# Values through two queues, short chunks on ScalarE, a reordered pool: one core's layernorm, attention and low-rank layer

## The chip, the cores and the metric

The kernel runs on one core of a Trainium2 chip. The metric is the time of one execution on the device in microseconds (us); lower is better. "The profile" is one execution recorded by the hardware profiler: a page of summaries, and a trace that can be asked about single engines, lines and stretches. Engines are called PE (TensorE, the matrix engine; PEld its weight loads), DVE (VectorE), ACT (ScalarE), POOL (GpSimd) and SP (SyncE, which here does nothing but issue transfers, called DMAs). A "q" behind the name (ACTq, SPq) marks what an engine's sequencer does itself, such as issuing a DMA.

## The reference

```
x  = hidden_states                      # 4 sequences, 512 tokens, 1024 wide, float32
xn = layernorm(x)
out = x + attention(xn) + lora(xn)

attention: qkv = xn @ w_qkv             # 32 query heads, 8 key/value heads, 128 wide
           scores = q.k * scale - slope[head] * sqrt(distance), causal
           out = softmax(scores) @ v, then @ w_o
lora:      xn @ W.T + b + (one of four nested ranks, chosen for each token
           by a gate's softmax) xn @ A[:r].T @ B[:, :r].T
```

All is computed in float32.

## The kernel before

The kernel has three stages. `project` (to about 1146 us) normalises the tokens, projects them to queries, keys and values, and in its gaps prepares sums of the output weights. `attend` (about 1146 us to 1765 us with the passage that follows it) computes the attention. `finish` multiplies attention's output and the normalised tokens by their weights and adds everything up. The large products of the first and the last stage follow a scheme of seven products in place of eight, on two levels (the functions named `inner`, `outer`, `Inner`, `Outer`); it is paid for with sums and differences of quarters of the operands, on DVE and POOL, and with scratch tensors in device memory (`s_d`, `t_d`, `m_d`, `c_d`).

**Order.** In `project` (after its start) PE, SP, DVE and POOL, and in `attend` all five engines, execute their instructions exactly in the order in which the program writes them. An instruction that waits therefore holds up everything behind it on its engine, and that goes for DMAs too: a DMA is an instruction of the engine that issues it, and it waits there.

**The weights' sums in `project`.** `weights_put_by` is a generator, three of which run by turns in slots of the projection (a slot is one call of `beside`, about one group of four products). It loads a piece through ACT's queue (`load`, L788, its DMAs at L794, L801 and L804), waits 8 slots (L822), issues four differences on POOL or DVE as slots are free (`busy`, L810), waits 4 slots (L829), issues the store on SP (L836) and waits 6 slots. The tiles are called `wr`. POOL also makes the sums of weights that PE is about to use (`ti_q`, `ti_kv`), in the same queue.

**Attention.** There are 32 units (2 pairs of sequences, 8 key/value heads, 2 sequences of a pair). A unit holds the 4 query heads of its group and takes 4 steps; the loop in L1217 runs T over 128 steps and some more. With n and q the unit and the quarter of step T, the steps do, in this order:

- `load` (q = 0, SP): keys and queries of unit n+1.
- `values` (q = 2, L1030): the values of unit n, four DMAs of 256 KB that put the same data on four groups of 32 partitions, all on SP (L1035). The tiles `vx` and `vy` alternate between units, so unit n's values take the place of unit n-2's.
- `distances` (q = 2, when a new head begins at unit n+1, which is at odd n): the bias, one activation on ACT (L1027).
- `settle` (q = 2, L1120): four copies on ACT (L1127) take unit n-2's products out of four PSUM banks into `o`. The same four banks hold the next unit's.
- `scores` (L1047): four products of queries and keys on PE (L1053, `psc`), for each DVE's bias and minimum (L1058) and ACT's exp with its sum (L1061). A step has two rows of queries, and each is cut in a long and a short chunk; `rows` (L1039) yields them as k = 0 to 3, the odd ones short (32 to 256 columns), the even ones long (512 to 288).
- `scaled` (L1071), for the step before: POOL multiplies the four chunks by the inverse sums.
- `turn` (L1077), for two steps before: DVE transposes the probabilities into `ptx` or `pty`.
- `weigh` (L1113), for six steps before: PE multiplies them with the values (L1100, `po`).
- `aside` (L1191): pieces of the sums over a finished pair's outputs. `outer_sums` makes `os` from `o`; `middle_sums` makes further sums in `ot1`, `ot5` or `ot7` and stores all to `s_d` by SP (L1172 to L1186). The sums named (1, 2), (5, 6, 3) and (7, 4) are for different products of the last stage.

At T = 112 (L1226) the first operands of the last stage are loaded by SP, and from T = 128 PE begins its first products.

**The passage.** The last pair (`last`) is summed by DVE and POOL after the loop (L1262 to L1272); its sums take the buffers `ot5` and `ot7` again, which must first have been stored for the pair before. Its (5, 6, 3) and (7, 4) sums are stored through POOL's queue (L1168).

**Buffers.** A pool lays its tiles out in the order in which they are first asked for (L1215 for attention's; its `p`, `vx` and `ptx` lie in a pool of their own). When attention's pool is closed, the last stage's pool `c2` (L1437 to L1445) takes the same memory, and a tile there must wait for the last user of the bytes below it. Counted in KB from the start of the pool, attention's order gives `o` 0 to 24, `ot7` to 30, `ot5` to 39, `os` (two) to 63, `ot1` to 71, `vy` to 79, `pty` to 97. The last stage's gives `x` 0 to 16, `btb`, `um` and `lw` to 30, `r4` (eight) to 62, `t4` (two) to 67, `u` (two) to 75, `m1`, `m5` and `m6` (two each) to 81, `wz` to 91. `u` holds the copies of the first four products (L1394), to which the next ones are added; `t4` is the fourth sum of weights (L1343).

Of the kernel before, what the change touches and what calls it, by code (L numbers as in the profile page):

```python
# [12 lines left out]
F32 = mybir.dt.float32  # L13
AF = mybir.ActivationFunctionType
ALU = mybir.AluOpType
# [7 lines left out]
P = 128  # L23
# [43 lines left out]
def kernel(  # L67
# [13 lines left out]
    nc = tc.nc  # L81
    B, S, H = x.shape
    DOUT = wt.shape[1]
# [3 lines left out]
    NP = B // 2  # L87
    HS = S // 2
    SCALE = D ** -0.5
    KB = 5  # L90
    C = P // G
# [273 lines left out]
    def project(attention):  # L365
# [5 lines left out]
        with pool("a") as sb, tc.tile_pool(name="stats", bufs=2, reuse_waits="tile") as stats:  # L371
# [20 lines left out]
            def buf(tag, name):  # L392
                where = ar if tag in ("w0", "x11", "xi1", "x12", "xi2") else sb
                return where.tile([P, *sizes[tag]], F32, tag=tag, name=name, bufs=counts.get(tag, 1))
# [110 lines left out]
            V, GP = nc.vector, nc.gpsimd  # L505
# [131 lines left out]
            def own_sums():  # L637
                return pace[2] - pace[5] in OWN
# [145 lines left out]
            def weights_put_by(turn):  # L784

                def load(key):  # L788
                    w = buf(f"wr{turn}", "wr_" + "_".join(str(k) for k in key))
                    if len(key) == 3:  # L790
                        kp, e, j = key
                        v = w.rearrange("p (k c) n -> p k c n", k=2)
                        for c in range(2):
                            pin(nc.scalar.dma_start(  # L794
                                out=v[:, :, c], in_=rows_of(kp, ds(c * S + j * HS, HS))[:, :, e]
                            ))
                    else:
                        kp, i = key
                        if i in SUMMED:
                            src = t_d[:, SUMMED[i], :, :, kp].rearrange("p e j n -> p (e j) n")  # L800
                            pin(nc.scalar.dma_start(out=w, in_=src))  # L801
                        else:
                            k, c = {1: (0, 0), 2: (1, 0), 3: (1, 1)}[i]
                            pin(nc.scalar.dma_start(  # L804
                                out=w.rearrange("p (e j) n -> p e (j n)", e=2),
                                in_=rows_of(kp, ts(c, S))[:, k],
                            ))
                    return w

                def busy(eng):  # L810

                    held = pace[2] > pace[4] if eng is GP else own_sums()
                    return held or taken.get(eng, -9) > pace[2] - 2

                yield from pause(9 * turn)
                for n in range(turn, len(pieces), 3):
                    key, eng = pieces[n], (GP, V)[n % 2]
                    if len(key) == 2 and key[1] in SUMMED:
                        while not put_by >= {(key[0], e, j) for e in range(2) for j in range(2)}:
                            yield  # L820
                    w = load(key)
                    yield from pause(8)  # L822
                    for k, u, v in ((0, 1, 0), (1, 3, 1), (3, 3, 0), (2, 2, 3)):
                        while busy(eng):
                            yield
                        taken[eng] = pace[2]
                        pin(sub(eng, w[:, k], w[:, u], w[:, v]))
                        yield
                    yield from pause(4)  # L829
                    if len(key) == 3:  # L830
                        kp, e, j = key
                        dst = t_d[:, :, e, j, kp]
                    else:
                        kp, i = key
                        dst = m_d[i][:, :, kp]
                    pin(nc.sync.dma_start(out=dst, in_=w))  # L836
                    put_by.add(key)
                    yield from pause(6)
# [5 lines left out]
            def pause(n):  # L844
                for _ in range(n):
                    yield
# [124 lines left out]
    def attend(front, begin):  # L971
# [3 lines left out]
        with ExitStack() as stack:  # L975
            sb, sp, sq = None, None, early.__enter__()
# [14 lines left out]
            def buf(tag, name):  # L991
                where = sq if tag in queries else sp if tag in passing else sb
                return where.tile([P, *sizes[tag]], F32, tag=tag, name=name, bufs=counts.get(tag, 1))

            Q, K, V, O, bias = {}, {}, {}, {}, {}
# [22 lines left out]
            for g in range(G):  # L1018
                nc.gpsimd.affine_select(
                    out=dist[ts(g, C)], in_=dist[ts(g, C)], compare_op=ALU.is_ge, fill=FAR,  # L1020
# [9 lines left out]
            def values(u):  # L1030
                p, h, bi = u
                V[u] = buf("v" + "xy"[bi], f"v_{label(u)}")
                src = v_d[2 * p + bi, h - h % 2][h % 2].rearrange("k g c d -> k (g c) d")
                for g in range(G):
                    nc.sync.dma_start(out=V[u][ts(g, C)], in_=src)  # L1035

            PR, TOT, PT, PO, OS = {}, {}, {}, {}, {}

# [31 lines left out]

            def scaled(T):  # L1071
                for k, row, n in rows(T):
                    nc.gpsimd.tensor_scalar(  # L1073
                        row, row, TOT[T][:, k : k + 1], 1.0, ALU.mult, ALU.mult
                    )

            def turn(T):  # L1077

# [53 lines left out]
            last = (NP - 1, NKV - 1)  # L1132
# [20 lines left out]
            def middle_sums(p, h, which, of, t, kept):  # L1153


                g = len(which)
                a = t.rearrange("p (g e) (r k) -> p g e r k", g=g, r=2) if of == "o" else t.rearrange(
                    "p g e (r k) -> p g e r k", r=2
                )
                a11, a12, a21, a22 = [a[:, :, e, r] for r in range(2) for e in range(2)]  # L1160
                n = f"{p}_{h}_{which[0]}"
                m = buf(f"ot{which[0]}", f"ot_{n}").rearrange("p (s g) k -> p s g k", g=g)
                s1, s2, s4 = [m[:, k] for k in range(3)]
                s3 = m[:, 3] if kept else a21
                eng = nc.gpsimd if of == "o" and not kept else nc.vector
                kb, kp = divmod(h + 2, KB)

                queue = nc.gpsimd if (p, h) == last and not kept else nc.sync  # L1168
                d = [s_d[i][:, :, p, kb, kp] for i in which]
                if kept:  # L1170
                    for k in range(g):
                        nc.sync.dma_start(out=d[k][:, 0:4:2], in_=a[:, k, :, 0])  # L1172
                        nc.sync.dma_start(out=d[k][:, 3], in_=a[:, k, 1, 1])
                add(eng, s1, a21, a22)
                yield
                sub(eng, s2, s1, a11)
                yield
                sub(eng, s4, a12, s2)
                yield
                sub(eng, s3, a11, a21)  # L1180
                for k in range(g):
                    if kept:
                        nc.sync.dma_start(out=d[k][:, 1], in_=s3[:, k])
                    else:
                        queue.dma_start(out=d[k][:, :4], in_=a[:, k].rearrange("p e r k -> p (e r) k"))
                    queue.dma_start(out=d[k][:, 4:], in_=m[:, :3, k])  # L1186
                yield

            beside, below = deque(), deque()

            def aside(steps, times):  # L1191
                while steps and times:
# [15 lines left out]
            sb = stack.enter_context(pool("b"))  # L1208
# [3 lines left out]
            ordered.__enter__()  # L1212
            strict[0] = True

            for tag in "o ot7 ot5 os ot1 p vx vy ptx pty".split():  # L1215
                buf(tag, f"lay_{tag}")
            for T in range(STEPS + 6):  # L1217
                n, q = divmod(T, NQ)
# [9 lines left out]
                if part == 0 and done >= 0:  # L1228
                    u = p, h, bi = units[done]
# [29 lines left out]
            settle(units[-1], slice(0, 1))  # L1259
            aside(below, 99)  # L1260
            p, h = last
            cuts = [(ALL, slice(HS, S)), (ALL, slice(0, HS))]  # L1262
            sums = outer_sums(p, h, nc.vector, cuts)
            for k in range(8):
# [11 lines left out]
    def rows_of(kp, col):  # L1276

        return wt_v[:, kp, :, :, col] if kp < 2 else wo_v[:, kp - 2, :, :, col]
# [7 lines left out]
    def pin(instruction):  # L1286
        return instruction if strict[0] else tc.keep_in_program_order(instruction)
# [132 lines left out]
    def finish(sb, homes, ops, begun):  # L1420
# [14 lines left out]


        for tags, shape, n in (  # L1437
            ("x", [NP, 2, HS], 4), ("btb", [DOUT], 1), ("um", [NP, S], 1), ("lw", [12, P], 1),
            ("r4", [2, NP, HS], 8), ("t4", [KB, P], 2), ("u", [2, NP, HS], 2),
            ("m1 m5 m6", [HS], 2), ("wz", [2 * KB, HS], 1), ("sa10z sa11z", [KB, HS], 1),  # L1440
            ("s2 s4", [KB, HS], 2), ("t3", [KB, P], 2),
        ):
            for tag in tags.split():
                rank = tag in ("btb", "um", "lw")
                sb.tile([RMAX + 1 if rank else P, *shape], F32, tag=tag, name=f"lay_{tag}", bufs=n)  # L1445
# [346 lines left out]
```

## Time and profile before

| | us |
|---|---|
| median of 3 runs | 2530.39 |
| lowest and highest | 2528.26, 2533.35 |
| the profiled execution, its own time | 2529.27 |
| its span, first to last instruction | 2527.5 |

| engine | busy us | share of the span | instructions |
|---|---|---|---|
| PE | 2450.1 | 97% | 16096 |
| DVE | 1802.9 | 71% | 3586 |
| ACT | 516.0 | 20% | 1558 |
| POOL | 1929.3 | 76% | 2078 |

The page has the span in 40 slices of 63 us each; a digit is the busy share of a slice in tenths, 9 meaning 90% or more. A row of an engine's order of time gives the start in us, the length in us, the engine, the line of the kernel, the operation, what it writes and reads, how many of one kind were merged, and in square brackets the idle time before it with what ended that. The mean clock that PE was granted is 0.991 of full speed in this execution; there are stretches with 0.50.

### The profile page before, as it was taken

The numbers are of one execution on the slowest core, as the hardware profiler recorded it, in microseconds if no ns is written. First come the engines' busy times: TensorE is split into PE (matmuls) and PEld (weight loads), VectorE is DVE, ScalarE is ACT, GpSimd is POOL, SyncE is SP. The second block draws the span as 40 slices with busy tenths as digits, with TensorE's granted clock in tenths as the row PEclk, the third lists the DMA queues.
The fourth block names the chain that finished last, engine by engine and source line by source line (L and its number), as shares of the span: only waits on it lengthen the run. The fifth ranks groups of instructions, "written<-read, shape, count | busy, mean of one in ns | idle before, by whom it ended". The sixth has DMA issues, their size and how long they took to land.

```text
span 2527.5 us, 44178 instructions
## 1 busy us (share of the span) xinstructions
PE 2450.1 (97%) x16096; PEld 2082.3 (82%) x16096; DVE 1802.9 (71%) x3586; ACT 516.0 (20%) x1558; POOL 1929.3 (76%) x2078
## 2 busy tenths in 40 slices
PE   7999999999999999999999999997999999999999
PEld 6878888888888888887777777775888888888887
DVE  7776677778666676757899998975765666656574
ACT  3111111110000000116666666641000000000000
POOL 4578787887688898875999999975775667747583
PEclk9999999999999999999999999998999999999999
DMA  4389998878977777746899999999887877879884
GB/s 146 109 246 318 281 323 253 271 220 245 323 226 241 217 243 223 247 136 183 248 319 326 319 331 320 321 304 356 317 317 268 327 288 289 307 267 329 312 325 149
DMA packets 513834, 681.90 MB, mean 270 GB/s; under 512 B 155817, under 2 KB 424489, under 8 KB 499410
## 3 DMA queue, kind: packets, MB, share of 16 engines
q1 hardware_dynamic: 441554, 591.64, 71.5%
q10 hardware_dynamic: 70752, 82.85, 9.9%
q0 software_dynamic: 1312, 4.59, 0.5%
q8 instruction: 128, 2.10, 0.3%
q14 instruction: 88, 0.72, 0.1%
HBM read 417.89 MB, written 261.10 MB: 269 GB/s over the span
## 4 chain that ended last, share of the span: by engine, by line
PE 67%; DMA 3%; POOL 2%; DVE 1%; SPq 1%; issue 1%; ACT 0%; ACTq 0%; DVEq 0%; POOLq 0%
PE pc L1371 16%; PE po L1100 11%; PE psc L1053 10%; PE pd L1371 8%; PE pc_q L569 7%; PE pa L1371 4%; PE pd_q L569 3%; PE pc_kv L569 3%; PE pa_q L569 2%; PE pd_kv L569 2%; DMA sa<-s 1%; PE pa_kv L569 1%; POOL t L140 1%; POOL ti_q L140 1%; PE pc L1635 1%
## 5 line engine op out<-in xcount | busy, mean ns | idle before, releaser
L1100 PE MATMUL po<-pt,v 32*128 32x256 f32 (+7 forms) x6144 | 300.1, 334 | 5.1 <-DMA v<-v 4.4
L1061 ACT ACTIVATE p<-p,low 128x512 f32<-128x512 f32 (+15 forms) x512 | 261.4, 517 | 203.7 <-DVE low L1058 195.7
L1100 PEld LDWEIGHTS po<-pt,v 32*128 32x128 f32 x6144 | 266.1, 186 | 36.3 <-issue 23.7
L1073 POOL TENSOR_SCALAR p<-p,tot 128x512 f32<-128x512 f32 (+15 forms) x512 | 264.3, 534 | 41.3 <-DVE tot L1069 40.8
L1053 PE MATMUL psc<-k,q 128*128 128x512 f32 (+15 forms) x1024 | 279.4, 417 | 3.0 <-DVE low L1058 2.5
L140 POOL TENSOR_TENSOR t<-w 128x640 f32<-128x640 f32 x95 | 187.9, 1978 | 120.9 <-DMA w<-m 54.6
L1058 DVE CUSTOM_DVE_ANT_0 p<-psc,bias 128x512 f32<-128x512 f32 (+15 forms) x512 | 205.6, 435 | 69.5 <-PE psc L1053 66.1
L1053 PEld LDWEIGHTS psc<-k,q 128*128 128x128 f32 x1024 | 171.5, 191 | 96.6 <-issue 55.8
L140 POOL TENSOR_TENSOR t<-w,t 128x640 f32<-128x640 f32 x95 | 194.8, 2051 | 33.9 <-PE pc L1371 30.2
L140 POOL TENSOR_TENSOR wr<-wr 128x256 f32<-128x256 f32 x220 | 174.6, 795 | 47.2 <-DMA wr<-in_w_o_dram 21.6
L569 PE MATMUL pc_q<-xi,ti_q 128*128 128x256 f32 x640 | 167.6, 385 | 3.0 <-DVE q L137 2.7
L1084 DVE STREAM_TRANSPOSE pt<-p 128x1088 f32<-128x1088 f32 x128 | 167.0, 1305 | 1.7 <-POOL p L1073 1.7
L140 POOL TENSOR_TENSOR ti_q<-w_q 128x256 f32<-128x256 f32 x128 | 105.3, 822 | 67.7 <-PE pc_q L569 37.4
L140 DVE TENSOR_TENSOR wr<-wr 128x256 f32<-128x256 f32 x220 | 139.5, 634 | 14.0 <-DMA wr<-in_wt_dram 9.1
L569 PEld LDWEIGHTS pc_q<-xi,ti_q 128*128 128x128 f32 x640 | 121.4, 192 | 24.3 <-issue 4.9
L569 PE MATMUL pd_q<-xi,ti_q 128*128 128x256 f32 x448 | 117.6, 386 | 14.6 <-POOL ti_q L140 14.6
L179 ACT COPY m<-pc 128x256 f32<-128x256 f32 x30 | 11.2, 372 | 564.1 <-PE pc L1371 545.1
L1371 PE MATMUL pc<-s,t 128*128 128x256 f32 x480 | 113.3, 384 | 10.5 <-DVE m L137 10.5
L140 POOL TENSOR_TENSOR ti_q<-to_q 128x256 f32<-128x256 f32 x96 | 76.8, 800 | 47.5 <-PE pc_q L569 45.0
L1371 PE MATMUL pc<-sa,w 128*128 128x256 f32 x480 | 112.1, 381 | 0.1
L1371 PEld LDWEIGHTS pc<-s,t 128*128 128x128 f32 x480 | 92.4, 193 | 23.6 <-issue 10.9
L1371 PE MATMUL pd<-s,t 128*128 128x256 f32 x480 | 111.5, 379 | 0.0
(344 smaller groups left out, 5731.1 us busy)
## 6 DMA issues: line engine op xcount, KB each, us to landing
sa<-s SPq DMA_DIRECT2D x98, 640.0 KB, 7.9
s<-ot SPq DMA_DIRECT2D x107, 384.0 KB, 6.1
m<-wr SPq DMA_DIRECT2D x70, 512.0 KB, 4.1
w<-m SPq DMA_DIRECT2D x28, 1280.0 KB, 8.1
w_q<-in_w_qkv_dram SPq DMA_DIRECT2D x16, 2048.0 KB, 11.3
q<-q SPq DMA_DIRECT2D x32, 1024.0 KB, 5.7
v<-v SPq DMA_DIRECT2D x128, 256.0 KB, 5.9
s<-os SPq DMA_DIRECT2D x45, 512.0 KB, 6.1
```

Of the source, the lines that this page charges most:

```text
L140: return eng.tensor_tensor(dst, u, v, ALU.subtract)
L179: nc.scalar.copy(dst, alike(src, dst))
L569: nc.tensor.matmul(dst, ops_w[m][:, c, :], XI[i][m][:, c, :], start=start and c == 0, stop=c == 1, skip_group_check=True,)
L1053: nc.tensor.matmul(sc[:, :n], Q[u][:, n // C - 1].rearrange("p g k -> p (g k)"), K[u][:, :n], start=True, stop=True,)
L1058: nc.vector.tensor_tensor_reduce(row, sc[:, :n], bias[p, h][:, S - n :], -SCALE, BIG, ALU.add, ALU.min, low)
L1061: nc.scalar.activation(row, row, AF.Exp, bias=low, scale=-1.0, accum_out=TOT[T][:, k : k + 1])
L1073: nc.gpsimd.tensor_scalar(row, row, TOT[T][:, k : k + 1], 1.0, ALU.mult, ALU.mult)
L1084: nc.vector.transpose(dst, PR.pop(T).rearrange("p s (t k) -> p s t k", k=C))
L1100: nc.tensor.matmul(PO[u, g][:, to : to + n * C].rearrange("p (n k) -> p n k", k=C), V[u][ts(g, C), b % G * NT + b // G], x[:, :, :C], star ...
L1371: nc.tensor.matmul(bk, w[:, k], x[:, k], start=start and k == 0, stop=stop and k == KB - 1, skip_group_check=True,)
L1635: nc.tensor.matmul(bk, low["w"][:, c, d], low["u"][:, p, ts(r, HS)], start=start, stop=False, skip_group_check=True,)
```

## The change

Six places change.

1. The pauses of `weights_put_by`: 10 slots instead of 8 between load and first difference, 2 instead of 4 between the last difference and the store.
2. `values`: the DMAs for g = 1 and g = 3 go out on ACT's queue, those for g = 0 and g = 2 stay on SP's.
3. `scaled`: the short chunks (odd k) are multiplied by ACT (an activation with a scale per partition), the long ones by POOL as before.
4. `middle_sums` of the last pair: for (5, 6, 3) and (7, 4) the sums lie in a tile called `spare`, which takes the place of `pty` after its last use, in place of `ot5` and `ot7`. Their stores go through ACT's queue for (7, 4) and SP's for (5, 6, 3), instead of POOL's.
5. Attention's pool is laid out in another order. By the sizes in the code this gives `o` 0 to 24, `os` to 48, `pty` to 66 (of which `spare` takes 15 KB, to 63), `vy` to 74, `ot7` to 80, `ot5` to 89, `ot1` to 97.
6. `btb` grows by 1 KB, which moves everything behind it in `c2` by as much: `r4` is 31 to 63, `t4` to 68, `u` to 76, `m1` to 78, `m5` to 80, `m6` to 82, `wz` to 92.

```diff
@@ weights_put_by
-                    yield from pause(8)
+                    yield from pause(10)
                     for k, u, v in ((0, 1, 0), (1, 3, 1), (3, 3, 0), (2, 2, 3)):
...
-                    yield from pause(4)
+                    yield from pause(2)
@@ values
                 for g in range(G):
-                    nc.sync.dma_start(out=V[u][ts(g, C)], in_=src)
+                    (nc.sync, nc.scalar)[g % 2].dma_start(out=V[u][ts(g, C)], in_=src)
@@ scaled
                 for k, row, n in rows(T):
-                    nc.gpsimd.tensor_scalar(
-                        row, row, TOT[T][:, k : k + 1], 1.0, ALU.mult, ALU.mult
-                    )
+                    by = TOT[T][:, k : k + 1]
+                    if k % 2:
+                        nc.scalar.activation(row, row, AF.Identity, scale=by)
+                    else:
+                        nc.gpsimd.tensor_scalar(row, row, by, 1.0, ALU.mult, ALU.mult)
@@ middle_sums
-                m = buf(f"ot{which[0]}", f"ot_{n}").rearrange("p (s g) k -> p s g k", g=g)
+                m = spare.pop(which[0]) if (p, h) == last and which[0] in spare else buf(
+                    f"ot{which[0]}", f"ot_{n}"
+                )
+                m = m.rearrange("p (s g) k -> p s g k", g=g)
...
-                queue = nc.gpsimd if (p, h) == last and not kept else nc.sync
+                queue = nc.scalar if (p, h) == last and not kept and of == "o" else nc.sync
@@ attend
-            beside, below = deque(), deque()
+            beside, below, spare = deque(), deque(), {}
...
-            for tag in "o ot7 ot5 os ot1 p vx vy ptx pty".split():
+            for tag in "o os pty vy ot7 ot5 ot1 p vx ptx".split():
                 buf(tag, f"lay_{tag}")
...
             aside(below, 99)
             p, h = last
+            rest = sb.tile([P, 15, HS], F32, tag="pty", name="spare")
+            spare.update({5: rest[:, :9], 7: rest[:, 9:]})
@@ finish
-            ("x", [NP, 2, HS], 4), ("btb", [DOUT], 1), ("um", [NP, S], 1), ("lw", [12, P], 1),
+            ("x", [NP, 2, HS], 4), ("btb", [DOUT + HS], 1), ("um", [NP, S], 1), ("lw", [12, P], 1),
```

## The prediction

> **What bounds the kernel now.** I read the slices first, then the stages, then the engines' order of time at the two places that decide. The page:
>
> ```profile
> PE   7999999999999999999999999997999999999999
> ACT  3111111110000000116666666641000000000000
> POOL 4578787887688898875999999975775667747583
> DMA  4389998878977777746899999999887877879884
> ```
>
> TensorE (PE) is full but for slice 28. The stages, in which the columns after the window are its length, PE, weight loads, VectorE, ScalarE, GpSimd, clock, DMA share, GB/s:
>
> ```profile
> 1206.00:1640.00 434.00, 434.00 (x5601) 338.40 (x5600) 392.45 (x1099) 268.47 (x912) 429.77 (x551) 1.00 1.00 312
> 1640.00:1765.00 125.00, 102.54 (x1043) 82.52 (x1041) 79.55 (x158) 36.35 (x119) 81.86 (x92) 0.90 1.00 328
> ```
>
> Steady attention (the first row) is bound by PE, with no idle time. GpSimd is as full by chance: no PE wait names it there. The second row, the end of attention and the passage to the last stage, holds 22 us of idle PE. So anything that holds PE back in the first row adds to the span one for one, and only the second row, and some gaps of the projection (60 to 1146 us, PE 1056.48 of 1086), can give time back.
>
> Where PE is next to waiting is seen at the settling (L1127), four copies of a unit's products out of PSUM. ScalarE, then PE:
>
> ```profile
> 1451.69 0.39 ACT L1061 ACTIVATE p<-p,low 128x128 f32<-128x128 f32 x1
> ...
> 1452.76 2.05 ACT L1127 COPY o<-po 128x512 f32<-128x512 f32 x4 [0.60 <-PE po L1100]
> 1454.67 0.65 ACT L1061 ACTIVATE p<-p,low 128x384 f32<-128x384 f32 x1
> ```
> ```profile
> 1450.35 2.40 PE L1100 MATMUL po<-pt,v 32*128 32x256 f32 x48
> 1452.68 2.10 PE L1053 MATMUL psc<-k,q 128*128 128x384 f32 x8
> 1454.71 2.46 PE L1100 MATMUL po<-pt,v 32*128 32x256 f32 x48
> ```
>
> PE ends a unit's weighted values at 1452.68; the copies run to 1454.81; PE wants the same four banks for the next unit at 1454.71, the fourth in its fourth product. The slack is nothing: what delays the copies delays PE.
>
> **The change, part by part.**
>
> *Values by turns.* Two of each unit's four loads (L1035) go from SyncE's queue to ScalarE's. values(units[n]) stands at the head of step 4n+2, before distances() and settle(), and ScalarE runs its instructions in that order. The new loads must wait until PE has read the old values (of unit n-2), which is the very end of po that the settling waits for. Behind them stand the bias (L1027, when n is odd), the four copies, the exps; behind the copies stands PE. The trace shows no such load on ScalarE; the nearest row is a pair of its weight loads:
>
> ```profile
> 519.85 0.92 ACTq L794 DMA_DIRECT2D wr<-in_w_o_dram  x2
> ```
>
> I take 0.90 us a pair. Below, SyncE's shortest is 0.302 each (0.68 with the gaps); above, SyncE's in the backlog of attention is 3.50 for four, 1.8 a pair. I stay near the first: ScalarE's queue is empty in attention. A cost of nothing is only possible if the pair goes out before PE is done; that is rival A. Where n is odd, the bias, today hidden behind PE's last products, comes after the pair too:
>
> ```profile
> 1643.03 0.71 ACT L1027 ACTIVATE bias<-dist,slope 128x512 f32<-128x512 f32 x1
> 1643.76 2.05 ACT L1127 COPY o<-po 128x512 f32<-128x512 f32 x4
> ```
>
> It takes 0.71, less the 0.09 by which neighbours overlap (the exp of 0.39 is followed after 0.30), less 0.04 that shows already (these copies begin 0.13 after PE's end at 1643.63, the others 0.09): it adds 0.58. Units 2 to 31 are concerned: 16 without a bias at 0.90 are 14.4; 14 with one (odd n, 3 to 29) at 1.48 are 20.7. **+35 us** (bounds: 30x0.68+14x0.58 = 29; 30x1.8+14x0.58 = 62). Each gap stays below 1.5, and such gaps didn't bring the half clock: after 1.49 us idle at 570.99 four products still took 1.03.
>
> *Short chunks on ScalarE.* Eight activations a unit, 32 to 256 columns. I price them by the exps of those sizes (306 ns to 495, mean 0.41): 3.2 us of a unit's 17.4, in which ScalarE works 10.8 now. They stand behind the exps of the next step; in the step before a settling they have 32 and 64 columns, some 0.45 us with overlap, and the exps end 0.5 us before PE (1452.17, 1452.68): nothing. VectorE's transpose, which reads them, comes a step later. GpSimd loses rows of 290 to 693 ns (32 to 256 columns; 114 us in all), which nobody waited for in the steady part: nothing. If this cover fails, each 0.1 us at a settling is 3 us.
>
> *The stall at step 118.* PE waited for values once, behind the first loads for the last stage and six stores on SyncE:
>
> ```profile
> 1643.63 2.10 PE L1053 MATMUL psc<-k,q 128*128 128x384 f32 x8
> 1650.18 6.91 PE L1100 MATMUL po<-pt,v 32*128 32x256 f32 x48 [4.44 <-DMA v<-v]
> 1657.02 3.90 PE L1053 MATMUL psc<-k,q 128*128 128x320 f32 x8
> ```
>
> It costs 4.44 idle, then 4.5 and 1.8 us at half the clock (granted 0.50 from 1652 to 1660): 10.7. After: SyncE issues two loads, not four (2.87 us become 1.4), and PE comes 0.9 later, so some 2.1 us of idle are left, with perhaps half of the slow clock's 6. **-6** (bounds 0 and -10.7).
>
> A rule speaks here. The Trainium skill, "TensorE: Matmul & The Clock Gate", section "Why this matters for your kernels", allows no idle gap over about 3 us; by it the shrunken gap would keep the full clock, and the sum would be 3 us lower. Another speaks against the move: "DMA: Bandwidth & Descriptors", section "Issuing engines are not separate DMA queues", says that a second issuing engine saves issue time alone, not transfer time. By it the values still land behind the same bytes (DMA share 1.00 here), the stall stays, and the sum is 6 higher. I go between, since the trace shows both queues long (issues of 2 to 5 us) and engines full.
>
> *Last pair's sums in the probabilities' buffer, pool reordered.* The passage now:
>
> ```profile
> 1745.78 4.20 PE L1371 MATMUL pc<-s,t 128*128 128x256 f32 x10 [10.51 <-DVE m L137]
> ...
> 1760.67 4.63 PE L1371 MATMUL pc<-sa10y,t 128*128 128x256 f32 x10 [6.38 <-DVE m L137]
> 1765.41 2.94 PE L1371 MATMUL pc<-sa,w 128*128 128x256 f32 x10
> ```
>
> The first wait is for u (L1394), held to 1744.80 by the store of ot1, whose place it takes. After, u lies on the values (free at 1721), but ScalarE first issues the (7,4) stores, which wait for GpSimd's four ot7 sums (1730 to 1736, then four issues, 1738), and m1 lies on ot7, whose last store lands at about 1740 (GpSimd waits for it at 1740.01 today): PE goes on at 1740.5, 5 earlier. The second wait is t4 on os (VectorE's product waits until 1759.45); t4 now lies on the probabilities and is free: gone. What is late next is the following product's load (sa, issued 1744.66, landed 1765.4, by the chain of waits). Before it 4.5 MB of stores and 3.2 MB of loads must pass either way. They now start without a hole (310 GB/s in 1735 to 1750, against 407 after 1750: some 4 us), but the 2.7 MB of (5,6,3) stand ahead of the loads on SyncE's queue, and PE would idle there some 10 us and start at half clock. **-4** (bounds -12: all but the time of the bytes; +5: the queue order loses more than the hole gives).
>
> *Pauses 8/4 to 10/2* (L822, L829). Each weight sum is issued two slots (two groups of four products, 2x0.86 us) later after its load, the store at the same slot. The waits that it bears on are GpSimd's 21.6 us for wr (once 12.5, which idled PE 7.67 us at 691 and halved the clock for 10.2) and VectorE's 4.54 at 129 (PE 3.23). Cut by 1.7 each, with the second's slow clock spared: 5. SyncE, which waits 138.5 us for GpSimd in these stores, waits longer, and its later loads with it. **-4** (bounds -18: both events gone; +8: one new stall like that at 691).
>
> The sum: 35 - 6 - 4 - 4 = +21 on the profiled execution's 2529.27: **2550 us**. That execution lies 1.1 below the median of the runs (2530.39), so I leave the number there.
>
> **Rivals.**
>
> A, *the settling isn't held* (faster): the pair of loads leaves ScalarE before PE's end, and only the gains are left: 2529.3 - 14 = 2515. It decides if the loads' wait is met, or their issue done, before 1452.7 in the row above. For it: ScalarE has 0.5 us free there. Against it: the loads wait for the same products as the copies, and SyncE is seen waiting for PE at L1035 15 times, 30.4 us.
>
> B, *issues slow as SyncE's in the backlog*: +62 in place of 35 and the same gains, 2529.3 + 62 - 14 = 2577; with short chunks late at a settling, more. For it: DMA share 1.00, and ScalarE's single issues reach 1.18 us at L794. Against it: their median is 0.46.
>
> C, *the added time is given back*: a slower PE lets the stores drain, so that the passage's idle and half clock (some 25 us) go with the stall's 10.7: 35 - 36 = -1, 2529 us. For it: DMA share 1.00 up to 1765. Against it: the passage is a chain of sums, stores and loads that starts when attention ends.
>
> **Chances.** The forecast 0.61 (its own range 2533 to 2570), A 0.16, B 0.12, C 0.11. A run can tell about 0.2% (5 us) from no change. Faster: A and a third of C, 0.20. Within: most of C and the forecast's lower edge, 0.09. Slower: the rest, 0.71. The range leaves out A's lower part (0.1) and B's upper (0.08): 2516 to 2580.
>
> **What would show it.** Right: PE waiting for ScalarE's o (L1127) at L1100, some 0.9 and 1.5 us by turns, 30 times; two issues of L1035 on ScalarE just ahead of each settling; a unit every 18.5 us instead of 17.4; fewer than 4 us idle for values at step 118; no wait of ScalarE for the store of ot at L1394. Wrong: units still 17.4 us apart (A); issues of over 1 us on ScalarE (B); PE nearly without idle time between 1650 and the last stage (C). A new wait of PE for GpSimd's ti in the projection would make the pauses' term wrong.

## The result, and the profile after

The changed kernel takes 2670.57 us in the median of 4 runs (2665.72 to 2674.51), the kernel before 2529.94 beside it: a ratio of 1.0553, 95% interval 1.0533 to 1.0574. It is slower by 5.5%, some 140 us. I had said 2550, and 2580 at most. The profiled execution of the changed kernel is the one of 2665.72 us, with a span of 2664.0. Below, line numbers are those of the kernel shown in each case; the changed kernel's are up to 7 higher than before's (the weighing is L1102 there, the settling L1129).

The slices of the page, after:

```profile
PE   7999999999999999999898989888699999999999
ACT  3111111101000101176565656552000000000000
POOL 4687887877788888745565656555466567755593
PEclk9999999999999999999898989899799999999999
DMA  4389998879878777466878787887988878878884
```

PE is no longer full in most of slices 20 to 29. In slices 20 to 26 POOL has fallen from 9 to 5 or 6, and the granted clock changes between 8 and 9. The stages (columns as in the prediction), steady attention and then its end with the passage:

```profile
1200.00:1640.00 440.00, 394.31 (x4428) 309.30 (x4424) 316.66 (x868) 262.52 (x882) 256.72 (x277) 0.90 0.77 246
1730.00:1905.00 175.00, 132.06 (x1334) 107.18 (x1333) 105.30 (x218) 59.58 (x198) 84.79 (x77) 0.86 0.84 277
```

In the first row PE, which had no idle time before, is idle for 46 of 440 us, its mean clock is 0.90, and it has done a fifth fewer products in the same time (10.1 per us against 12.9). The transfers are less busy, not more: 0.77 of the engines' time against 1.00. So nothing is short of bandwidth; something holds PE. By stage, from the starts and ends of PE's products in the two traces:

| stretch | before, us | after, us | difference |
|---|---|---|---|
| up to the first `psc` of attention | 1140.8 | 1133.2 | -7.6 |
| attention, first `psc` to last `po` | 580.7 | 716.0 | +135.3 |
| last `po` to PE's last product | 801.5 | 810.4 | +8.9 |

Nearly all of it lies in attention. The waits of PE and of ACT (what waited, for what: us in all, times, longest):

```profile
PE po L1102 <- ACT o L1129: 70.8, 17, 6.4
PE pc L1378 <- DMA sa<-s: 15.1, 1, 15.1
```
```profile
ACT bias L1027 <- DMA s<-ot: 71.2, 13, 6.1
```

The first is the wait for the settling that I expected, but at 4 to 6 us a time and not at 0.9 and 1.5. The last names what ACT waited for ahead of it: a *store* of sums, which neither the bias nor the settling reads. Two units in ACT's order of time, an even one and the odd one behind it:

```profile
1428.27 0.78 ACTq L1035 DMA_DIRECT2D v<-v  x2
1429.15 2.06 ACT L1129 COPY o<-po 128x512 f32<-128x512 f32 x4 [1.13 <-PE psc L1053]
1446.61 5.22 ACTq L1035 DMA_DIRECT2D v<-v  x2
1451.88 0.72 ACT L1027 ACTIVATE bias<-dist,slope 128x512 f32<-128x512 f32 x1 [5.51 <-DMA s<-ot]
1452.51 2.03 ACT L1129 COPY o<-po 128x512 f32<-128x512 f32 x4
```

In the even unit the two loads take 0.78, a little less than the 0.90 that I had priced. In the odd unit they take 5.22, and the bias and the copies stand behind them. PE beside it:

```profile
1430.09 3.47 PE L1102 MATMUL po<-pt,v 32*128 32x256 f32 x48
...
1446.40 2.10 PE L1053 MATMUL psc<-k,q 128*128 128x384 f32 x8
1453.13 5.39 PE L1102 MATMUL po<-pt,v 32*128 32x256 f32 x48 [4.62 <-ACT o L1129]
```

After the even settling the weighing takes 3.47 in place of 2.46: 1.0 later. After the odd one PE is idle for 4.62, and then the same 48 products take 5.39, of which 1453 to 1456.9 at half the clock (granted 0.50). What the second load waited for is told by the chain of what ended last, and by SP's order of time:

```profile
1445.99 1.18 DVE ot L140
1447.17 0.02 issue
1447.18 0.32 SPq L1188
1447.50 0.04 issue
1447.55 3.96 DMA s<-ot
1451.50 0.02 issue
1451.52 0.31 ACTq L1035
```

DVE ends the last of the (1, 2) sums, SP stores them, and when the store has landed (1451.50) ACT's second load goes out (1451.52). The trace's semaphore events show why. Every DMA of SP and ACT raises, when it lands, one of eight semaphores (counters that an engine can wait for), which in these kernels are given out in turn over both queues; and an issue first waits until the DMA before it on the same semaphore has landed. The store issued at 1447.55 raises number 100. ACT's second load also raises number 100, and waits for it. The two have nothing to do with each other; they are eight transfers apart in the order in which the numbers are given out. That order is not the text's: `values` writes its four loads one behind the other, but ACT's two have numbers 116 and 100 here, with two of SP's stores (117 and 118) between them. In the last 14 of the 16 odd units it is this store (L1191) that the second load follows, and in each of the 14 the load goes out 0.02 us after the store has landed.

**Theory 1**, then: a load moved to ACT's queue brings along a wait for an older transfer of SP's, through the shared semaphore; in odd units that transfer is a store just issued; ACT's order puts the settling behind it; and a gap of 4 us makes PE run at half clock after it. Rivals: **2**, the pool's new order (`vy` beside other tiles) makes the wait; **3**, the short chunks make ACT late; **4**, two issues on ACT, or the traffic of two queues, cost this by themselves.

### The profile page after: what moved, and what is told of

Read it like the earlier page. It is cut to its first block, busy times and chain, and to the rows that moved or that the text cites. A ratio compares the mean times of both kernels' runs of the same rounds, so it can differ in the third digit from the quotient of the medians.

```text
span 2664.0 us, 44380 instructions
## 1 busy us (share of the span) xinstructions
PE 2516.1 (94%) x16096; PEld 2137.2 (80%) x16096; DVE 1807.2 (68%) x3586; ACT 595.7 (22%) x1814; POOL 1795.6 (67%) x1812
## 4 chain that ended last, share of the span: by engine, by line
PE 65%; DMA 5%; DVE 3%; SPq 2%; POOL 1%; issue 1%; ACT 1%; ACTq 0%; POOLq 0%; DVEq 0%
PE pc L1378 15%; PE po L1102 11%; PE psc L1053 8%; PE pd L1378 7%; PE pc_q L569 7%; PE pa L1378 4%; PE pd_q L569 3%; PE pc_kv L569 3%; DMA s<-ot 2%; PE pa_q L569 2%; PE pd_kv L569 2%; DVE pt L1086 1%; PE pa_kv L569 1%; DVE p L1058 1%; DMA sa<-s 1%
## 5 line engine op out<-in xcount | busy, mean ns | idle before, releaser
L1102 PE MATMUL po<-pt,v 32*128 32x256 f32 (+7 forms) x6144 | 357.6, 357 | 70.9 <-ACT o L1129 70.8
L1102 PEld LDWEIGHTS po<-pt,v 32*128 32x128 f32 x6144 | 316.3, 200 | 111.8 <-ACT o L1129 82.2
L1077 POOL TENSOR_SCALAR p<-p,tot 128x512 f32<-128x512 f32 (+7 forms) x256 | 150.7, 602 | 237.9 <-DVE tot L1069 225.2
L1053 PE MATMUL psc<-k,q 128*128 128x512 f32 (+15 forms) x1024 | 290.2, 429 | 3.0 <-DVE low L1058 2.5
L1053 PEld LDWEIGHTS psc<-k,q 128*128 128x128 f32 x1024 | 177.9, 197 | 99.8 <-issue 60.3
L1378 PEld LDWEIGHTS pc<-sa,w 128*128 128x128 f32 x480 | 92.0, 193 | 28.0 <-issue 15.5
```

Of the source, the lines that this page charges most:

```text
L1053: nc.tensor.matmul(sc[:, :n], Q[u][:, n // C - 1].rearrange("p g k -> p (g k)"), K[u][:, :n], start=True, stop=True,)
L1077: nc.gpsimd.tensor_scalar(row, row, by, 1.0, ALU.mult, ALU.mult)
L1102: nc.tensor.matmul(PO[u, g][:, to : to + n * C].rearrange("p (n k) -> p n k", k=C), V[u][ts(g, C), b % G * NT + b // G], x[:, :, :C], star ...
L1378: nc.tensor.matmul(bk, w[:, k], x[:, k], start=start and k == 0, stop=stop and k == KB - 1, skip_group_check=True,)
```

## The experiments

**Values alone.** Before, with one line changed:

```diff
-                    nc.sync.dma_start(out=V[u][ts(g, C)], in_=src)
+                    (nc.sync, nc.scalar)[g % 2].dma_start(out=V[u][ts(g, C)], in_=src)
```

> The kernel before with the values by turns alone (two of each unit's four value loads on ScalarE's queue), nothing else changed. Theory 1: in every odd unit ScalarE's second load waits for the landing of a store that SyncE issued late, because both use the same completion semaphore; this stands ahead of the settling, and PE, after 4 us or more of idleness, runs at half clock. It needs none of the other edits: about 15 gaps of 4 to 6 us at the weighing of odd units, and 2530 + 135 to 140, 2660 to 2675 us. Rival 2 (the new order of the pool makes the wait): no long gaps, 2550 to 2570. Rival 3 (the short chunks on ScalarE make it late): the same, 2550 to 2570.

Measured: 2671.44 us, ratio 1.0554 (1.0538 to 1.0569). This one line is the whole loss. PE's waits:

```profile
PE po L1100 <- ACT o L1127: 72.5, 17, 7.0
```

Rivals 2 and 3 fall, as this kernel has neither the new pool order nor the short chunks.

**All but the values.** The changed kernel with the old line in `values`.

```diff
-                    (nc.sync, nc.scalar)[g % 2].dma_start(out=V[u][ts(g, C)], in_=src)
+                    nc.sync.dma_start(out=V[u][ts(g, C)], in_=src)
```

> The changed kernel with all value loads back on SyncE's queue; the other edits stay. Theory 1: no gap of over 2 us at the weighing, attention as long as before or a few us shorter; 2530 - 7.6 (projection) + 7 (passage) - 0 to 6 (stall at step 118) = 2522 to 2532 us. Rivals 2 and 3 (pool order or short chunks): most of the loss stays, 2600 to 2660.

Measured: 2533.59 us, ratio 1.0003 (0.9994 to 1.0013), 1.6 us above my upper end. PE is busy for 440.00 of 440.00 us of steady attention. The other edits together are worth nothing; the stretches say how (-4.2 up to attention, +2.5 in it, +5.9 behind it).

**Values behind the settling.** The changed kernel with `values(units[n])` moved below `settle(u)` in the same step: same loads, same queues.

```diff
                 if q == 2 and n < len(units):
-                    values(units[n])
                     if n + 1 < len(units) and units[n + 1][2] == 0:
...
                         below.append(of_pair(p, h, nc.gpsimd, HEADS))
+                if q == 2 and n < len(units):
+                    values(units[n])
                 if T < STEPS:
                     scores(T)
```

> The changed kernel with the values of a unit issued right behind the settling of the unit before it instead of ahead of it: the same four loads on the same two queues, moved past four copies. Theory 1: PE no longer waits for the copies out of the banks; ScalarE still waits for an older transfer's landing, now ahead of the exponentials, which PE needs only some steps later, so most of the 135 us comes back: 2530 to 2590 us, gaps at the weighing under 2 us. Rival 4 (the loss comes from the two queues' traffic itself, not from what stands behind the issue): 2640 to 2680.

Measured: 2562.96 us, ratio 1.0121 (1.0102 to 1.0140). PE's waits there:

```profile
PE pc L1379 <- DMA sa<-s: 14.4, 1, 14.4
...
PE psc L1053 <- DVE low L1058: 10.6, 8, 7.0
PE po L1102 <- ACT o L1129: 5.1, 9, 0.8
```

The wait for the settling falls from 70.8 to 5.1. ACT still stands between its loads (the two issues are seen apart, at 1428.78 and 1434.23, for example), but now the exps are behind them, which PE needs later. 108 of the 137 us come back by the place of the loads in ACT's order alone, so the traffic is not the cause of these. The other 29 I haven't divided.

**One load.** The changed kernel with only g = 1 on ACT's queue. In odd units its load then comes, on its semaphore, after a load of keys.

```diff
-                    (nc.sync, nc.scalar)[g % 2].dma_start(out=V[u][ts(g, C)], in_=src)
+                    (nc.scalar if g == 1 else nc.sync).dma_start(out=V[u][ts(g, C)], in_=src)
```

> The changed kernel with one of the four value loads of a unit on ScalarE's queue (the second group) instead of two. By the order of the transfers on the eight completion semaphores this one load follows a load of keys, landed long before, in odd units too. Theory 1: ScalarE pays only the issue, about 0.45 us a unit, 30 x 0.45 = 14 us over the version with all on SyncE, 2535 to 2550 us, and no gap of over 2 us at the weighing of odd units. Rival 4 (each transfer on this queue costs a share of the loss, as issue or as traffic): about half of the 135 us stays, 2590 to 2610.

Measured: 2558.71 us, ratio 1.0108 (1.0091 to 1.0125). Half of the loads cost 25 us, not half of 137: rival 4's equal shares fall. My figure was too low too. The distances between settlings give the reason: half of the pairs of units take 36.3 us against 35.0 with all on SP (some 19 in 15 pairs), the others up to 1.4 more, and one gap of 7.7 stands near the end. The last two are the same wait. I had taken the load of keys as landed long before, but in the slowest pair it landed at 1480.43, 1.4 us after PE's products had ended, and ACT's load went out at 1480.57. At the gap of 7.7 ACT's load followed a load of weights for the last stage, which landed at 1654.08 (issue 1654.14).

**Earlier stores.** The changed kernel, loads untouched; DVE's (1, 2) sums get two turns in the two steps from the even settling on:

```diff
-                aside(beside, 1 if T < STEPS else 4)
+                aside(beside, (2 if part < 2 and done % 2 == 0 else 1) if T < STEPS else 4)
```

> The changed kernel, all its loads on the same two queues in the same place ahead of the settling; only the four sums that DVE makes behind the settling of an even unit, with their four stores, are given out two steps in a row at twice the pace, so that the stores are issued about two steps (9 us) earlier. In the order of the transfers ScalarE's two loads of an odd unit then follow, on their semaphores, a store landed by then and a load of keys. Theory 1: no gap of over 2 us at the weighing of odd units, no half clock behind them; what stays is the issue of two loads ahead of each settling, 24 (measured for one load a unit) to 50 us over the version with all on SyncE: 2558 to 2584 us. Rival 4 (two queues' traffic, or two issues on ScalarE, make the gaps): 2640 to 2675.

Measured: 2591.85 us, ratio 1.0252 (1.0237 to 1.0268). ACT's two loads of an odd unit, at the same place ahead of the settling:

```profile
1456.92 0.79 ACTq L1035 DMA_DIRECT2D v<-v  x2
1457.76 0.72 ACT L1027 ACTIVATE bias<-dist,slope 128x512 f32<-128x512 f32 x1 [1.09 <-PE psc L1053]
1458.39 2.03 ACT L1129 COPY o<-po 128x512 f32<-128x512 f32 x4
```

0.79 in place of 5.22, and no gap of 4 us in the steady part (one of 5.7 stands at step 114, where ACT's second load follows a load of queries that landed at 1681.68 and goes out at 1681.70). No load was touched, only the turns of sums and stores that the loads have nothing to do with. As these moved, the pairing moved too: here the first load follows a store landed at 1453.05, the second a load of keys landed at 1457.00, 0.27 before it went out. Two issues on ACT and two queues are still there; with the older transfers landed, the wait is gone. So it is the landing that the load waits for. The total is 8 us above my upper end: PE now waits 10.0 us (8 times) for queries, `psc` for `q<-q`, because the earlier stores stand ahead of those on SP, and the odd settlings keep some lateness.

**Even units alone, odd units alone.** The changed kernel, ACT's queue used only where `bi` is 0 (all else on SP), and only where it is 1:

```diff
-                    (nc.sync, nc.scalar)[g % 2].dma_start(out=V[u][ts(g, C)], in_=src)
+                    (nc.sync, nc.scalar)[g % 2 * (1 - bi)].dma_start(out=V[u][ts(g, C)], in_=src)
```
```diff
-                    (nc.sync, nc.scalar)[g % 2].dma_start(out=V[u][ts(g, C)], in_=src)
+                    (nc.sync, nc.scalar)[g % 2 * bi].dma_start(out=V[u][ts(g, C)], in_=src)
```

> The changed kernel with the values by turns in even units alone; odd units load all four on SyncE. In even units ScalarE's two loads follow loads that landed long before. Theory 1: 15 settlings later by two issues, 0.9 to 1.0 us each: 14 to 15 us over the version with all on SyncE, 2545 to 2552 us; no gap of over 2 us. Rival 4 (each load on this queue costs an equal share): half of the 137 us, about 2602.

Measured: 2618.95 us, ratio 1.0349 (1.0331 to 1.0368). A miss: 85 us over all on SP, not 15. The even units, harmless in the changed kernel, are not here:

```profile
1485.88 2.92 ACTq L1035 DMA_DIRECT2D v<-v  x2
1488.89 2.05 ACT L1129 COPY o<-po 128x512 f32<-128x512 f32 x4 [3.27 <-DMA q<-q]
```

Their second load follows, on its semaphore, the load of queries for the odd unit. I had taken that as landed long before. But the odd unit's four value loads now stand ahead of it on SP: it was issued at 1479.85 and landed nearly 9 us later. It is the same wait for another transfer; which one it is, and how late, depends on every DMA in between.

> The changed kernel with the values by turns in odd units alone; even units load all four on SyncE. By the order of the transfers ScalarE's second load of 14 odd units still follows the store of the sums made behind the settling just before. Theory 1 with the half clock: each of these settlings is later by the wait (4.3 us more than the 0.8 of two issues) and the halved weighing behind it (about 3 us), some 8 a pair: 14 x 8 = 112 us over the version with all on SyncE, 2635 to 2655 us, with gaps of 4 to 6 us at the weighing of odd units and a record of half clock behind each. Rival 4 (each load on this queue costs an equal share of the 137 us): about 2602.

Measured: 2662.50 us, ratio 1.0520 (1.0498 to 1.0541), 7.5 us above my upper end. The odd units alone cost 129 us over all on SP. PE waits for the settling 80.9 us (16 times, the longest 7.4). The halves don't add up to 137 (85 + 129), since each kernel has its own pairing of transfers; how the changed kernel's own loss divides is read from its own trace, below.

**The other edits, each alone,** on the kernel before. First the short chunks:

```diff
+                    by = TOT[T][:, k : k + 1]
+                    if k % 2:
+                        nc.scalar.activation(row, row, AF.Identity, scale=by)
+                    else:
+                        nc.gpsimd.tensor_scalar(row, row, by, 1.0, ALU.mult, ALU.mult)
```

> The kernel before with the short chunks scaled on ScalarE alone. Theory 1: ScalarE and POOL both have room, PE's order is untouched: within 4 us of before, 2528 to 2536; if the stall at the value load of step 118 came from POOL, it goes and the time is 2524 to 2528. Rival 3 (the copies make ScalarE late ahead of the settling): 2550 or more.

Measured: 2532.22 us, ratio 1.0009 (1.0000 to 1.0018): nothing to 0.2% slower. From an even settling to the next odd one it takes 17.7 us in place of 17.4: there two short chunks (1435.59 to 1436.14, for example) stand ahead of the bias, and the copies begin at 1436.65, 0.48 after PE's end and not 0.13. That is 0.3 in 15 places, partly made up at the end of attention.

The pauses:

```diff
-                    yield from pause(8)
+                    yield from pause(10)
...
-                    yield from pause(4)
+                    yield from pause(2)
```

> The kernel before with the pauses of the weight sums changed from 8 and 4 to 10 and 2, alone. The changed kernel's trace has the first product of attention 7.6 us earlier than before, the version with all values on SyncE 4.2 us earlier; no other edit acts ahead of it. If that is this edit's: 4 to 8 us faster, 2524 to 2528. If it is the spread from run to run: 2530 to 2534.

Measured: 2523.27 us, ratio 0.9973 (0.9964 to 0.9982). The pauses are worth 7 us. The first `psc` comes at 1134.1 instead of 1140.8. The wait of PE at 691 falls from 7.67 to 5.57, and its half clock from 10.2 us to 3.4; but a wait at 663 (2.15 us, 0.43 before) has 3.4 us of half clock of its own.

The last pair's parts (4 to 6 of the change), of which the core is

```diff
+            spare.update({5: rest[:, :9], 7: rest[:, 9:]})
...
-                queue = nc.gpsimd if (p, h) == last and not kept else nc.sync
+                queue = nc.scalar if (p, h) == last and not kept and of == "o" else nc.sync
...
-            for tag in "o ot7 ot5 os ot1 p vx vy ptx pty".split():
+            for tag in "o os pty vy ot7 ot5 ot1 p vx ptx".split():
```

> The kernel before with the last pair's parts alone: its sums in the turned probabilities' buffer, attention's pool reordered, its (5,6,3) stores on SyncE's queue and its (7,4) stores on ScalarE's instead of all on POOL's. In the version with all values on SyncE the stretch behind the last weighing was 5.9 us longer than before, with SyncE's first load of the next operands 8.5 us later behind six more stores. If that is these parts': 5 to 7 us slower, 2535 to 2538 us, with a wait of 13 to 15 us for sa<-s. My prediction's term (the buffers free the sums early): 4 us faster, 2526.

Measured: 2537.35 us, ratio 1.0030 (1.0018 to 1.0043), 7 us slower. In that kernel the passage has

```profile
1747.44 4.60 PE L1376 MATMUL pc<-s,t 128*128 128x256 f32 x10 [10.32 <-DVE m L137]
1772.46 2.90 PE L1376 MATMUL pc<-sa,w 128*128 128x256 f32 x6 [13.94 <-DMA sa<-s]
```

The first wait has stayed (10.51 before), and the second has grown from 6.38 to 13.94, now for operands.

**The last pair's stores on POOL's queue again** (with the pauses, without values and short chunks):

```diff
-                queue = nc.scalar if (p, h) == last and not kept and of == "o" else nc.sync
+                queue = nc.gpsimd if (p, h) == last and not kept else nc.sync
```

> The kernel before with the pauses (10 and 2) and the last pair's buffers and pool order, but the last pair's (5,6,3) and (7,4) stores on POOL's queue, as before. If the loss behind the last weighing comes from SyncE's queue (six stores ahead of the next operands' loads), it goes, and the earlier sums may bring the first wait down: 2515 to 2524 us, against 2523.3 of the pauses alone. If it comes from the buffers or the pool's order: 2528 to 2532.

Measured: 2530.56 us, ratio 1.0008 (0.9999 to 1.0017), 7 us more than the pauses alone, as much as the last pair's parts lost with the other queues. So in time the choice of queue made no difference; what it did was to move the wait:

```profile
1734.57 3.79 PE L1376 MATMUL pc<-s,t 128*128 128x256 f32 x10 [5.46 <-DVE m L137]
1766.09 4.63 PE L1376 MATMUL pc<-sa,w 128*128 128x256 f32 x10 [21.26 <-DMA sa<-s]
```

The buffers do free the sums: the first wait is 5.46. But SP's first load of the next operands (`sa10z`) goes out only at 1752.55, though the last store ahead of it on SP was issued at 1736.6. In the program its wait is for the stores from `ot1`, whose place it takes in the new order.

**Another pool order.** As the last one, with `ot1` first:

```diff
-            for tag in "o os pty vy ot7 ot5 ot1 p vx ptx".split():
+            for tag in "ot1 o os pty vy ot7 ot5 p vx ptx".split():
```

> As the run before (pauses, last pair's buffers, its stores on POOL's queue), but attention's pool begins with ot1, so that the tile of the next operands' first load no longer lies where the (1,2) sums wait for their stores; this load then follows, in its own semaphore alone, a store made early. If the 21 us wait came from that place in memory: SyncE's loads start where they do in the version with the pauses alone, or up to 5 us earlier, the first wait of PE stays at 5.5 and the second falls to 6 to 11: 2517 to 2524 us. If it came from POOL's queue or from the sums: 2528 to 2532 again.

Measured: 2528.35 us, ratio 0.9985 (0.9976 to 0.9994), in the range that I had given for POOL's queue or the sums as the cause. The place in memory did make that wait, since `sa10z` is issued at 1739.24 now. But `u` has come to lie on `spare`:

```profile
1752.16 0.37 ACT L1399 COPY u<-pa_begun 128x256 f32<-128x256 f32 x1 [35.23 <-DMA s<-spare]
1752.43 0.38 ACT L1399 COPY u<-pb_begun 128x256 f32<-128x256 f32 x1
```

PE has one wait of 23.49 us instead of 5.46 and 21.26. In the three layouts and two choices of queue tried, the passage's two waits sum up to 17 us (the kernel before) to 27: what one arrangement frees, another early tile waits for. None beats the kernel before there. The best kernel of this study is the one with the pauses alone, 2523.27 us.

## Why the prediction was wrong, step by step

**Values by turns, +35: wrong, and the whole error.** The step that failed is "The new loads must wait until PE has read the old values": I took this as their only wait. What I priced is there. The first pair of settlings after the changed kernel's start, before the late store comes into play, is 2.2 us longer than with all on SP (18.9 and 18.3 against 17.7 and 17.3), which would be 33 us in 15 pairs, and two issues take 0.78 as against my 0.90. But a load also waits for the last transfer on its semaphore. I saw the nearest row, a pair of weight loads on ACT at 0.92, and bounded it by SP's issues in a backlog (1.8), as if a long issue were slow work. And I kept near the lower end because ACT's queue was empty, which doesn't help when the semaphore is shared with SP's. SP's long issues are another thing: between 1206 and 1640 of before, each of the 146 of over 0.9 us began after the transfer ahead of it on its semaphore had landed, 135 of them more than 1 us after. So neither bound came from a row with this wait, and on ACT it can be as long as a store takes to be issued and to land. Measured: 4.8 to 5.6 us for the two loads of an odd unit, and 137 us in place of 35 for the term. My rival B went in this direction, but with 1.8 a pair.

**"Each gap stays below 1.5, and such gaps didn't bring the half clock": wrong as a consequence.** Right for gaps of that size (below), but the gaps were of 4 to 6 us. In the steady part a pair of units takes 44.5 us in the changed kernel and 35.0 with all on SP. Of the 9.5, 2.2 are the issues, 4.4 the longer wait (5.2 less 0.8), and the remaining 2.9 are what the weighing at half clock takes more (5.39 in place of 2.46).

**Short chunks, 0: about right.** Measured 0 to 0.2% slower. I looked at the exps' end before the settling, and missed that where n is odd the bias stands between: with half a microsecond more ahead of it, the copies come 0.35 later against PE's end.

**The stall at step 118, -6: not shown.** The distance between the two settlings there is 28.1 us before, 26.4 with the short chunks, 26.1 with the pauses, 28.7 with the last pair's parts and 26.4 with all on SP. In the changed kernel the stall for `v<-v` is gone, but one unit earlier, at step 114, ACT's two loads take 6.28 us behind the first loads for the last stage, and PE waits 6.40 for the settling. I can't tell a gain of the edit from this spread.

**Last pair and pool, -4: wrong in sign, +7.** I had both effects, and "PE would idle there some 10" was measured at 13.94. Two gains failed. ACT's four stores were to be issued by 1738; with the last pair alone they start at 1742.47 (1738.4 with all on SP) and take 3.8 us in all, and `u` is copied behind them, so the first wait keeps its length. And the second wait, for `t4`, is gone, but the loads behind it come later by more: `sa10z` is issued at 1754.19 there, behind the six stores, and at 1741.45 before. My upper bound of +5 was for the second effect alone.

**Pauses, -4: right in sign, measured -7, and only in part where I had put it.** Both waits that I had named were cut: product by product, PE gains 3.4 at 134 and 2.1 at 699 in the profiled executions. But it loses 2.6 at 139 and 2.2 at 668 to waits beside them, and 3.4 of the gain lie at 269 and 571, which I hadn't named.

The Trainium skill, "DMA: Bandwidth & Descriptors", section "Issuing engines are not separate DMA queues", says that a second issuing engine saves no transfer time. I weighed it only at the stall; it spoke to the whole edit. Here the engines' busy share even fell, from 1.00 to 0.77.

## What to carry to other kernels

A DMA issued from a compute engine is an instruction of that engine with all of the DMA's waits, and among them is the landing of whatever transfer last used its completion semaphore, on any queue. Before a load is moved to such an engine, see in a trace which transfer stands one round of the semaphores ahead of it and when that one lands (the text's order doesn't tell), and see what is behind the load in the engine's order; put it behind the work that the bottleneck waits for. And when buffers are laid out anew, look for the stores still under way below each early tile of the next stage: freeing one wait here only moved it.

## What the hardware showed that I had not expected

- In all the kernels here the semaphores are eight for SP and ACT together, in turn from the first DMA to the last; whether other programs get eight isn't shown. A pair of issues of one kind on one engine took 0.78 us, 2.92 and 5.22 in these kernels, by what stood eight transfers ahead.
- How large a gap brings PE's half clock. In attention and the passage of all fourteen kernels, each of the 86 gaps seen at 2.5 us or more has a record of half clock that begins at most 1.4 us after the gap's end, and of 3.4 to 23.9 us; the gaps between 1.0 and 1.5 have none. Between 1.5 and 2.5 it is mixed: 1.57, 1.63 and 2.40 without one in the kernel with the earlier stores; 1.96 and 2.28 with one in the same kernel, and 1.53 to 2.43 with one in the kernel with the even units by turns, where behind 2.12 the 48 products took 5.40. The Trainium skill, "TensorE: Matmul & The Clock Gate", section "Why this matters for your kernels", puts the limit at about 3 us; here a seen gap of about 2 was often enough. Part of a wait can lie in a row counted as busy, so the true gaps may be a little longer.
- A slower PE left the other engines and the transfers emptier (POOL 429.77 busy of 434 before, 256.72 of 440 after), and none of this came back as time: behind attention the changed kernel took 8.9 us more, not less.
